# A two-layer image network on one core: layer 1's experts and final pass of three images placed within the last image's sampling

## The chip, the core and the metric

The kernel is one program on one core of a Trainium2 chip. The core has TensorE (PE, matrix products and transposes; its loads of the stationary operand are listed as PEld), VectorE (DVE), ScalarE (ACT), GpSimd (POOL) and SyncE (SP). Each has its own queue of instructions and runs it strictly in order. Memory transfers are issued from queues of SP, ACT and POOL and carried out by 16 DMA engines. The metric is the device time of one execution in microseconds (us), median over runs; lower is better. The profile is of one execution.

## The reference

The input is four images x of 128 channels by 128 x 128 pixels, all float32. There are two layers, each a convolution step and a mixture-of-experts step, both with residuals.

```
# layer 0
x = x + deform_conv(norm_over_channels(x))       # 9 taps, each at a learned offset, bilinear: 4 corners per tap
t = tokens(x)                                    # 16384 tokens of 128 per image
t = t + moe2(layernorm(t))                       # 8 experts, softmax router, the best 2 of each token
# layer 1
x = x + fourier_conv(norm_over_channels(x))      # real part of ifft2 of a channel mix of fft2
t = tokens(x)
z = layernorm(t)
probs = softmax(z @ gate_w.T + gate_b, over the 16384 tokens)      # 64 experts
topv, topi = the 8 tokens of largest probs, for each expert
pooled[e] = sum_k topv[k,e] * z[topi[k,e]]
out[e] = gelu([pooled[e],1] @ weight1[e]) ; out[e] = [out[e],1] @ weight2[e]   # 129x512 and 513x128 per expert
t[topi[k,e]] += topv[k,e] * out[e]               # scatter-add of 512 rows per image
x = image(t)                                     # back to channel-major
```

In layer 1 experts choose tokens, so no expert of an image can be run before all 16384 tokens of the image have been through the layers ahead of it. weight1 and weight2 are 16.8 MB each. The Fourier convolution reduces to x + A * (x flipped in both axes), and the kernel computes it so: `flip` and `aT_sb`.

## The kernel before, in words

**Sampling.** For each image a table in DRAM is built (`Image`, `block`, `positions`), whose row for a pixel holds the normalised pixel and its lower neighbour. One row read at a position, together with the next row, then gives all four corners of a bilinear sample. `Chunk.gather` issues three indirect DMAs on POOL for one image row and three taps; `weighted` multiplies the samples by the bilinear weights on DVE (`weighted_too` does the third tap of some chunks on ACT); `summed` adds the corners while transposing on PE (`trg`); `convolved` multiplies by the convolution weights (`sums`). A group is four image rows: two near the top and the two that mirror them, as the flip needs. It has 12 chunks. An image has 32 groups, thus 384 chunks, and the four images have 1536.

**Mixing.** `mixed` carries a group through layer 0's router and experts, the Fourier convolution, layer 1's layernorm and gate, and writes the tokens x2 to DRAM (`x2_d`). Of each run of tokens it keeps the best eight logits of each expert with their places (`best`, `best_at`). Experts of an even image lie in partitions 0 to 63, of an odd one in 64 to 127 (`gwT_sb[:, h]`), and `chosen(p)` picks the eight tokens of each expert for a pair of images, once the pair's second image is done.

**The order of work.** It is written out by hand. `InOrder` (its line, L83, is the line of every instruction that goes through it) keeps each engine's instructions in program order. `Turns` is a small cooperative scheduler that runs while the program is written: one slot per chunk, and jobs (generators) which say after how many slots they go on (`yield 1`, `yield turns.hop`), or wait for a free PSUM bank (`yield FILL`, at most `BANKS` = 6 over two adjacent slots). A chunk takes a bank itself. `turns.hop` is 2 while chunks run and 1 at the end: the slots between a matmul and the use of its result. Chunks are gathered `AHEAD` = 7 slots before they are summed, and there are as many gather buffers. While an image is sampled, the table of the next one is built (jobs `table_of`). In the last image's slots there is no table to build. SP carries the loads of x (`xc`, `xg`), the table writes (`table<-ent`) and the writes of x2.

**Behind the sampling.** When all slots are done, and the mixing of the last group too, comes straight-line code with pools of its own. `Pair` gathers the chosen tokens of two images (16 indirect DMAs, L1064), normalises and sums them weighted by their probabilities (L239, L1077, L1081), and puts them into `poolT`. The experts run once for all four images: 16 chunks of four experts. `first_layer` loads 1 MB of weight1 and four blocks of weight2 and multiplies (`ph`, L1165); `transposed` turns the hidden units and applies bias and gelu (`trh`, L1179); `second_layer` multiplies by weight2 (`po`, L1199); `turned` turns the outputs back (`pt`, L1211). Between them `Pair.equal` computes `share`, which for each chosen row adds up the weights of all experts that chose the same token (L1094 to L1105), so that rows chosen twice are written with the same sum. `Pair.give` adds the outputs to the gathered tokens and scatters them into `x2_d` (L1128). The final pass reads x2 in 64 tiles of 512 KB, transposes them (`pf`, L1248), copies them from PSUM on DVE and ACT and writes out (`ob`), the reads issued from SP, the writes from ACT.

Of the kernel before, what the change touches and what calls it, by code (L numbers as in the profile page):

```python
# [48 lines left out]
P = 128  # L50
NB = 4
# [6 lines left out]
TOPK = 8  # L58
TAPS = 9
# [5 lines left out]
TC = P + 2  # L65
AHEAD = 7
# [29 lines left out]
class Turns:  # L96
# [10 lines left out]
    def start(self, job, wait=0):  # L107
        self.jobs.append([job, self.slot + wait, False])
# [20 lines left out]
    def fills(self, spare):  # L129

        for one in self.jobs[:]:
            while one[2]:
                taken = sum(self.filled.get(self.slot - i, 0) for i in range(self.hop))
                if taken + spare >= BANKS or self.filled.get(self.slot, 0) + 2 >= BANKS:
                    return
                self.fill()
                if not self.resume(one):
                    break
# [30 lines left out]
def metaformer_kernel(  # L169
# [31 lines left out]
    x2_d = [dram.tile([2 * NTOK, P], F32, name=f"x2_d{p}") for p in range(NB // 2)]  # L201

    def x2_cols(b):

        half = x2_d[b // 2][b % 2 * NTOK : (b % 2 + 1) * NTOK, :]
        return half.rearrange("(x y) c -> x (y c)", y=P)
# [4 lines left out]
    best = [const.tile([P, RUNS, TOPK], F32, name=f"best{p}") for p in range(NB // 2)]  # L211
    best_at = [const.tile([P, RUNS, TOPK], U32, name=f"best_at{p}") for p in range(NB // 2)]

    token = [const.tile([P, TOPK], F32, name=f"token{p}") for p in range(NB // 2)]
    index = [const.tile([P, TOPK], I32, name=f"index{p}") for p in range(NB // 2)]
    val = [const.tile([P, TOPK], F32, name=f"val{p}") for p in range(NB // 2)]
    iota = const.tile([P, RUNS * TOPK], F32, name="iota")
    nmax = [const.tile([P, P // 4], F32, name=f"nmax{p}") for p in range(NB // 2)]
    esum = [const.tile([P, P // 4], F32, name=f"esum{p}") for p in range(NB // 2)]

    def rstd_of(pool, mv, n, eps, tag):

        r = pool.tile([P, n], F32, name=f"{tag}_rs", tag=f"{tag}_rs")
        nc.scalar.activation(r, mv[:, :, 1], AF.Sqrt, bias=eps)
        nc.vector.reciprocal(r, r)
        return r

    def layernorm(pool, src, dst, n, eps, tag):

        st = pool.tile([P, n, 6], F32, name=f"{tag}_st", tag=f"{tag}_st")  # L230
        mv = pool.tile([P, n, 2], F32, name=f"{tag}_mv", tag=f"{tag}_mv")
        for i in range(n):
            nc.vector.bn_stats(st[:, i, :], src(i))
            nc.vector.bn_aggr(mv[:, i, :], st[:, i, :])
        r = rstd_of(pool, mv, n, eps, tag)
        nb = pool.tile([P, n], F32, name=f"{tag}_nb", tag=f"{tag}_nb")
        nc.vector.scalar_tensor_tensor(nb, mv[:, :, 0], -1.0, r, ALU.mult, ALU.mult)
        for i in range(n):
            nc.scalar.activation(  # L239
                dst(i), src(i), AF.Identity, bias=nb[:, i : i + 1], scale=r[:, i : i + 1]  # L240
            )

    with ExitStack() as main:
        wts = main.enter_context(tc.tile_pool(name="wts", bufs=1))
        pa = main.enter_context(tc.tile_pool(name="pa", bufs=2))
        pt = main.enter_context(tc.tile_pool(name="pt", bufs=1))
        pw = main.enter_context(tc.tile_pool(name="pw", bufs=2))
        pg = main.enter_context(tc.tile_pool(name="pg", bufs=AHEAD))
        pb = main.enter_context(tc.tile_pool(name="pb", bufs=2))
        p_x = main.enter_context(tc.tile_pool(name="p_x", bufs=BANKS, space=PSUM))  # L250
# [13 lines left out]
        class Image:  # L264
# [23 lines left out]
            def border(self):  # L288
# [3 lines left out]
                    in_=zeros.rearrange("p (j e) -> p j e", j=2),  # L292
# [3 lines left out]
                    in_=zeros[0:1].rearrange("p (j e) -> p j e", j=2),  # L296
# [23 lines left out]
        zeros = wts.tile([P, 4 * P], F32, name="zeros")  # L320
# [8 lines left out]
        gwT_sb = wts.tile([P, 2, 2 * E1], F32, name="gwT_sb")  # L329
        nc.vector.memset(gwT_sb, 0.0)  # L330
        gb_sb = wts.tile([P, 1], F32, name="gb_sb")
        for h in range(2):
            nc.sync.dma_start(out=gwT_sb[:, h, h * E1 : (h + 1) * E1], in_=gate_w)
# [377 lines left out]
        def mixed(group):  # L711
# [7 lines left out]
            x1 = pb.tile([P, 4, P], F32, name="x1", tag="x1", bufs=5)  # L719
# [151 lines left out]
            p, h = divmod(b, 2)  # L871
            half = slice(h * E1, (h + 1) * E1)
            pq = bank([P, 4, P], "pq")
            eng.tensor.matmul(pq, lhsT=gwT_sb[:, h, :], rhs=tn2T, start=True, stop=True)
# [4 lines left out]
            eng.scalar.activation(lq[half], pq[half], AF.Identity, bias=gb_sb[half])  # L879
            yield 1  # L880
            tops = [best[p][half, (y + 1) // 2, :] for _, y, _ in runs]
            for i, (s, y, n) in enumerate(runs):
                run = lq[half, s : s + n, :].rearrange("p s c -> p (s c)")
                eng.vector.max(out=tops[i], in_=run)
                eng.vector.max_index(
                    out=best_at[p][half, (y + 1) // 2, :], in_max=tops[i], in_values=run
                )
            g = slice(group.number, group.number + 1)
            low = nmax[p][half, g]
            eng.vector.tensor_tensor(low, tops[0][:, 0:1], tops[1][:, 0:1], ALU.max)  # L890
            eng.vector.tensor_scalar(low, low, -1.0, None, ALU.mult)
            last = h == 1 and group.number + 1 == len(groups)
            exps.append((lq[half], low, esum[p][half, g], p if last else None))
# [4 lines left out]
        def exponentials():  # L898

            while exps:  # L900
                logits, low, total, pair = exps.pop(0)
                eng.scalar.activation(logits, logits, AF.Exp, bias=low, accum_out=total)
                if pair is not None:
                    turns.start(chosen(pair), 1)
# [391 lines left out]
```

## Time and profile before

| | us |
|---|---|
| median of 3 runs (6427.51 to 6435.13) | 6430.69 |
| the profiled execution's own time | 6432.53 |
| its span, first to last instruction | 6430.5 |
| busy PE / DVE / ACT / POOL over the span | 5722.3 / 5408.9 / 3801.4 / 4398.7 |
| mean granted TensorE clock | 0.957 of full |
| moved by DMA | 1488.42 MB, mean 231 GB/s |

How to read it: "busy" is the time in which an engine has an instruction in execution; issuing a DMA isn't counted, save for the indirect ones on POOL (`DMA_INDIRECT`), which show with their time of issue. In a row by stretch of time each engine has its busy time with the number of its instructions. In a row of waits come the instruction that waited, what released it, the total time, the number and the longest. "issue" as the releaser means that the profile shows nothing that the engine waited for. In a timeline row come the start, the duration, the engine, the line, the instruction, its count, and in brackets the idle time before it with its releaser. In a row of DMA issues come the destination and source, the queue, the number, the size and the median time from issue to landing.

The stages: the first image's table until about 150, the sampling of four images with the table of the next one beside it until about 6036, the last groups' mixing until about 6131, then choice, experts, scatter and final pass to 6430.5.

### The profile page before, as it was taken

The page shows a single profiled execution, that of the slowest core. Times are in us where ns is not written, and L with a number is a line of the kernel's source. Part 1 is how long each engine was busy: PE and PEld are TensorE (multiplying, and loading weights), DVE is VectorE, ACT ScalarE, POOL GpSimd, SP SyncE. Part 2 cuts the span into 40 slices and gives each one's busy share as a digit, 9 for nine tenths or more (in the row PEclk, how much of TensorE's full clock was granted, in tenths as well). Part 3 has the DMA queues.
Part 4 walks back from the last instruction along what each step waited for, and adds up shares of the span by engine and source line. Part 5 has one row for each costly group of instructions (what it writes and reads, how often), then busy time and mean ns, then how long its engine had stood idle before and what let it go on. Part 6 is the DMA issues. An engine that isn't in the chain of part 4 may idle for free.

```text
span 6430.5 us, 101708 instructions
## 1 busy us (share of the span) xinstructions
PE 5722.3 (89%) x30863; PEld 3750.9 (58%) x30863; DVE 5408.9 (84%) x16007; ACT 3801.4 (59%) x10144; POOL 4398.7 (68%) x4653
## 2 busy tenths in 40 slices
PE   8789999999899999999899999999888888888746
PEld 3456666666566666666565656666555555555425
DVE  5579988899899999899889998999888888888862
ACT  5456666665566666666566666666555555555522
POOL 0577777777777777777777777777777777777410
PEclk8899999999999999999999999999999999999976
DMA  4677877777777778777777777777777777777649
GB/s 138 198 238 242 249 236 237 234 226 224 237 243 243 240 242 249 225 227 226 238 244 237 243 239 237 239 236 226 220 224 220 224 223 221 224 221 224 201 160 405
DMA packets 580527, 1488.42 MB, mean 231 GB/s; under 512 B 84840, under 2 KB 251600, under 8 KB 579984
## 3 DMA queue, kind: packets, MB, share of 16 engines
q0 software_dynamic: 369664, 1210.35, 63.1%
q1 hardware_dynamic: 200944, 237.85, 10.8%
q10 hardware_dynamic: 9376, 33.72, 1.3%
q8 instruction: 250, 4.10, 0.3%
q14 instruction: 293, 2.40, 0.1%
HBM read 1344.74 MB, written 136.85 MB: 230 GB/s over the span
## 4 chain that ended last, share of the span: by engine, by line
PE 33%; DVE 33%; DMA 19%; issue 6%; ACT 4%; POOL 4%; POOLq 0%; SPq 0%; DVEq 0%; ACTq 0%
DMA g<-table,index 16%; PE trg L83 12%; DVE g L83 11%; DVE x L83 10%; PE sums L83 7%; PE pe L83 5%; PE po L83 5%; POOL g L83 4%; PE tr L83 2%; DMA out<-ob 2%; ACT ent L83 1%; DVE c_st L83 1%; DVE best_at L83 1%; ACT g L83 1%; PE ps L83 1%
## 5 line engine op out<-in xcount | busy, mean ns | idle before, releaser
L83 POOL DMA_INDIRECT g<-table,index x4608 | 4364.2, 947 | 1665.7 <-issue 836.0
L83 PEld LDWEIGHTS trg<-ident,g 128*128 128x128 f32 x18432 | 2132.4, 143 | 1157.4 <-issue 676.2
L83 PE MATMUL trg<-ident,g 128*128 128x128 f32 x18432 | 2359.5, 278 | 290.0 <-issue 117.2
L83 DVE TENSOR_TENSOR g<-g,spread 128x1024 f32<-128x1024 f32 (+1 forms) x1536 | 2136.2, 1392 | 346.7 <-DMA g<-table,index 312.6
L83 DVE SCALAR_TENSOR_TENSOR x<-pe,scaled,x 128x128 f32<-128x128 f32 x4096 | 1424.8, 348 | 196.7 <-PE pe L83 85.8
L83 ACT ACTIVATE g<-g,weight 128x128 f32<-128x128 f32 x4096 | 1306.9, 392 | 457.8 <-DMA g<-table,index 260.6
L83 PE MATMUL sums<-sT,wconv_sb 128*128 128x512 f32 x2304 | 1216.9, 610 | 0.2
L83 PE MATMUL pe<-ew_sb,x1T 128*128 128x512 f32 x2048 | 1087.9, 614 | 111.7 <-ACT sT L83 64.5
L83 ACT COPY sT<-trg 128x384 f32<-128x384 f32 x1536 | 713.0, 467 | 612.0 <-PE trg L83 608.9
L83 PEld LDWEIGHTS sums<-sT,wconv_sb 128*128 128x128 f32 x2304 | 406.7, 194 | 427.1 <-issue 424.4
L83 PEld LDWEIGHTS pe<-ew_sb,x1T 128*128 128x128 f32 x2048 | 318.8, 193 | 213.6 <-ACT sT L83 84.2
L83 PE MATMUL po<-pad,woff_sb 128*54 128x512 f32 x768 | 373.0, 627 | 7.4 <-ACT pad L83 5.0
L83 ACT ACT_TABLE_LOAD x264 | 338.7, 1283 | 22.0 <-DMA rw_sb<-in_router_w 8.4
L83 ACT ACTIVATE xn<-x,c_nb,c_rs 128x128 f32<-128x128 f32 x512 | 210.6, 483 | 111.2 <-DVE c_nb L83 111.0
L83 ACT ACTIVATE ent<-raw,a_nb,a_rs 128x128 f32<-128x128 f32 x512 | 210.6, 484 | 70.7 <-DVE a_nb L83 69.4
L83 ACT ACTIVATE tn<-x,d_nb,d_rs 128x128 f32<-128x128 f32 x512 | 211.0, 485 | 55.1 <-DVE d_nb L83 55.1
L83 PE MATMUL sums<-xg,ident 128*128 128x512 f32 x256 | 151.3, 675 | 97.5 <-ACT x1T L83 97.2
L83 PEld LDWEIGHTS po<-pad,woff_sb 128*54 128x54 f32 x768 | 93.8, 134 | 208.2 <-issue 189.8
L83 DVE BATCH_NORM_STATS2 a_st<-raw 128x6 f32<-128x128 f32 x512 | 137.5, 268 | 51.9 <-ACT raw L83 51.9
L83 ACT ACTIVATE e<-e 128x4 f32<-128x4 f32 x128 | 26.3, 206 | 259.8 <-DVE e L83 259.2
L1248 PE MATMUL pf<-ident,xt 128*128 128x128 f32 x512 | 114.2, 389 | 67.2 <-DVE ob L1250 33.6
L83 ACT COPY os<-po 54x512 f32<-54x512 f32 x128 | 74.1, 579 | 159.4 <-PE po L83 159.1
(208 smaller groups left out, 5310.0 us busy)
## 6 DMA issues: line engine op xcount, KB each, us to landing
g<-table,index POOLq DMA_INDIRECT x4608, 3.7
table<-ent SPq DMA_DIRECT2D x64, 1024.0 KB, 6.2
xc<-in_x SPq DMA_DIRECT2D x64, 512.0 KB, 6.7
xt<-x_d SPq DMA_DIRECT2D x64, 512.0 KB, 7.2
out<-ob ACTq DMA_DIRECT2D x64, 512.0 KB, 7.8
xg<-in_x SPq DMA_DIRECT2D x124, 256.0 KB, 5.4
x_d<-x SPq DMA_DIRECT2D x124, 256.0 KB, 4.0
w<-in_weight SPq DMA_DIRECT2D x16, 1024.0 KB, 8.8
```

The costliest lines, as they stand in the source:

```text
L83: return self.tc.keep_in_program_order(issue(*args, **kwargs))
L1248: nc.tensor.transpose(pf[:, i, :], xt[:, 4 * g + i, :], ident)
```

## The change

The token choice is made per image. The gate's weights stand in both halves of the stationary operand, so that both halves of the partitions hold the 64 experts' logits of the same image. Of an expert's best eight tokens the lower half keeps the first four and the upper half the last four (`KEPT`), so one indirect DMA still moves 128 rows, and an image needs four of them.

The code behind the sampling becomes jobs of the same scheduler, marked `later`: they get a free PSUM bank only after the others. `Experts` holds a set of images: `taken` gathers and pools, `network` runs both layers with one gelu between them, `give` scatters, `sent` is the final pass. One `Experts` for images 0 to 2 starts with the last image's first slot, in the space of the closed pools of the table building, with two buffers of 1 MB for weights and then for the final pass's tiles (`depth` 2, a first layer every two slots, `pace`). A second one, for image 3, starts when the last chunk is done, with nine such buffers in the space of the sampling's pools, and reads the weights again. `lead` spaces POOL's and the tiles' instructions by slots as long as chunks run, and sends the outputs by SP instead of ACT. weight2 is read in rows of 2 KB instead of 512 bytes: hidden unit number 4p + j is now in place (p, j). The buffers of x1 go from five to four, and the table's borders are zeroed from a source that is read twice.

```diff
+KEPT = TOPK // 2
+EC = 4
+NC = E1 // EC
+LATE = NB - 1
...
+    def start(self, job, wait=0, later=False):
+        self.jobs.append([job, self.slot + wait, False, later])
...
-        for one in self.jobs[:]:
+        for one in sorted(self.jobs, key=lambda one: one[3]):
...
+    x2_d = [dram.tile([NTOK, P], F32, name=f"x2_d{b}") for b in range(NB)]
...
+        phase_a, sampling = (main.enter_context(ExitStack()) for _ in range(2))
+        pa = phase_a.enter_context(tc.tile_pool(name="pa", bufs=2, side="right"))
+        pt = phase_a.enter_context(tc.tile_pool(name="pt", bufs=1, side="right"))
         pb = main.enter_context(tc.tile_pool(name="pb", bufs=2))
+        pw = sampling.enter_context(tc.tile_pool(name="pw", bufs=2))
+        pg = sampling.enter_context(tc.tile_pool(name="pg", bufs=AHEAD))
...
+        gwT_sb = wts.tile([P, 2 * E1], F32, name="gwT_sb")
...
-            x1 = pb.tile([P, 4, P], F32, name="x1", tag="x1", bufs=5)
+            x1 = pb.tile([P, 4, P], F32, name="x1", tag="x1", bufs=4)
...
+            eng.scalar.activation(lq, pq, AF.Identity, bias=gb_sb)
...
+            for h in range(2):
+                half, mine = slice(h * E1, (h + 1) * E1), slice(h * KEPT, (h + 1) * KEPT)
+                eng.vector.tensor_copy(place[half], i8[half, mine])
+                eng.vector.tensor_copy(top[half], m8[half, mine])
...
+        class Weights:
+            def __init__(self, room):
+                self.room, self.tiles, self.loaded = room, {}, 0
+            def load(self, upto):
+                while self.loaded < min(upto, 2 * NC):
+                    i = self.loaded
+                    layer, c = divmod(i, NC)
+                    some = slice(c * EC, (c + 1) * EC)
+                    self.tiles[i] = self.room(i)
+                    eng.sync.dma_start(
+                        out=self.tiles[i],
+                        in_=weight2[some, 0:HID, :].rearrange("e (p j) o -> p e (j o)", j=NJ)
+                        if layer
+                        else weight1[some, 0:P, :].rearrange("e d h -> d e h"),
+                    )
+                    self.loaded += 1
...
+            def lead(self):
+                return AHEAD + 2 if turns.hop > 1 else 0
+            def start(self):
+                turns.start(self.inputs(), later=True)
+                turns.start(self.network(), later=True)
...
+            def taken(self, b):
+                while b not in known:
+                    yield 1
+                yield self.lead()
+                tok = self.tok[b] = late.tile([P, KEPT, P], F32, name=f"tok{b}", tag=f"tok{b % LATE}", bufs=1)
+                for k in range(KEPT):
+                    eng.gpsimd.indirect_dma_start(
+                        out=tok[:, k, :],
+                        out_offset=None,
+                        in_=x2_d[b],
+                        in_offset=bass.IndirectOffsetOnAxis(ap=index[b][:, k : k + 1], axis=0),
+                    )
+                if self.lead():
+                    yield 4
...
+                eng.vector.tensor_tensor(
+                    tn, tn, val[b].unsqueeze(2).to_broadcast([P, KEPT, P]), ALU.mult
+                )
+                sum4 = late.tile([P, P], F32, name="sum4", tag="one")
+                eng.vector.tensor_reduce(sum4, tn.rearrange("p k c -> p c k"), AX.X, ALU.add)
+                yield 1
...
+                for k in range(KEPT):
+                    wide = late.tile([P, P], F32, name="wide", tag="one")
+                    eng.vector.tensor_copy(wide, token[b][:, k : k + 1].to_broadcast([P, P]))
+                    yield 1
+                    yield FILL
+                    along = bank([P, P], "along")
+                    eng.tensor.transpose(along, wide, ident)
+                    yield turns.hop
+                    same = late.tile([P, P, KEPT], F32, name="same", tag="two")
+                    eng.vector.tensor_tensor(
+                        same,
+                        along.unsqueeze(2).to_broadcast([P, P, KEPT]),
+                        token[b].unsqueeze(1).to_broadcast([P, P, KEPT]),
+                        ALU.is_equal,
+                    )
+                    eng.vector.tensor_tensor(
+                        same, same, val[b].unsqueeze(1).to_broadcast([P, P, KEPT]), ALU.mult
+                    )
+                    eng.vector.tensor_reduce(share[:, k, :], same, AX.X, ALU.add)
...
+                def first_layer(c):
+                    while c not in weights.tiles:
+                        yield 1
+                    yield FILL
+                    ph = bank([P, HID], "ph")
+                    w1 = weights.tiles.pop(c)
+                    for e in range(EC):
+                        at = m * (c * EC + e)
+                        eng.tensor.matmul(
+                            ph[32 * e : 32 * e + 32, :],
+                            lhsT=self.given[:, at : at + 32],
+                            rhs=w1[:, e, :],
+                            start=True,
+                            stop=True,
+                        )
+                    yield turns.hop
+                    weights.load(c + 1 + self.depth)
+                    hidden = late.tile([P, HID], F32, name="hidden", tag="hidden")
+                    eng.scalar.copy(hidden, ph)
...
+                def second_layer(c):
+                    while NC + c + 1 not in weights.tiles:
+                        yield 1
+                    yield FILL
+                    po = bank([P, 2, P], "po2")
+                    for i in range(2):
+                        w2 = weights.tiles.pop(NC + c + i)
+                        for j in range(NJ):
+                            for e in range(EC):
+                                at = m * ((c + i) * EC + e)
+                                eng.tensor.matmul(
+                                    po[32 * e : 32 * e + 32, i, :],
+                                    lhsT=self.units[:, j, at : at + 32],
+                                    rhs=w2[:, e, j * P : (j + 1) * P],
+                                    start=(j == 0),
+                                    stop=(j == NJ - 1),
+                                )
+                    yield turns.hop
+                    weights.load(NC + c + 2 + self.depth)
...
+                for c in range(NC):
+                    turns.start(first_layer(c), later=True)
+                    yield self.pace
+                while len(done) < NC:
+                    yield 1
+                some = self.units[:, :, 0 : E1 * m]
+                eng.scalar.activation(some, some, AF.Gelu)
+                yield 1
+                for c in range(0, NC, 2):
+                    turns.start(second_layer(c), later=True)
+                    yield 2 * self.pace
+                while len(done) < NC + NC // 2:
+                    yield 1
+                for b in self.bs:
+                    turns.start(self.give(b), later=True)
+                    yield self.pace
+                while len(done) < NC + NC // 2 + m:
+                    yield 1
+                tiles = [(b, t) for b in self.bs for t in range(P // RB)]
+                for i in range(self.depth):
+                    turns.start(self.sent(tiles[i :: self.depth]), later=True)
...
+            def sent(self, tiles):
+                for b, t in tiles:
+                    io = self.weights.room(t)
+                    xt, ob = io[:, 0:2, :], io[:, 2:4, :]
+                    some = slice(t * RB * P, (t + 1) * RB * P)
+                    eng.sync.dma_start(
+                        out=xt.rearrange("p i c -> p (i c)"), in_=x2_cols(b)[:, some]
+                    )
+                    done = []
+                    def part(g):
+                        yield FILL
+                        pf = bank([P, HID], "pf")
+                        for i in range(4):
+                            some = slice(i * P, (i + 1) * P)
+                            eng.tensor.transpose(pf[:, some], xt[:, g, some], ident)
+                        yield turns.hop
+                        if g == 0:
+                            eng.scalar.copy(ob[:, g, :], pf)
+                        else:
+                            eng.vector.tensor_copy(ob[:, g, :], pf)
+                        done.append(g)
+                    if self.lead():
+                        yield 2
+                    for g in range(2):
+                        turns.start(part(g), later=True)
+                    while len(done) < 2:
+                        yield 1
+                    if self.lead():
+                        yield 1
+                    (eng.sync if self.lead() else eng.scalar).dma_start(
+                        out=out_cm[b, :, some], in_=ob.rearrange("p i x -> p (i x)")
+                    )
...
+            if n == LATE * slots:
+                phase_a.close()
+                late = main.enter_context(tc.tile_pool(name="late", bufs=2, side="right"))
+                b1T = late.tile([P, NJ, E1], F32, name="b1T", tag="b1T", bufs=1)
+                b2T = late.tile([P, E1], F32, name="b2T", tag="b2T", bufs=1)
+                turns.start(biases(), later=True)
+                room = lambda i: late.tile([P, EC, HID], F32, name="w", tag="w")
+                weights = Weights(room)
+                weights.load(2)
+                Experts(range(LATE), weights, 2, 2).start()
...
+                sampling.close()
+                own = main.enter_context(tc.tile_pool(name="own", bufs=OWN))
+                room = lambda i: own.tile([P, EC, HID], F32, name="w", tag="w")
+                weights = Weights(room)
+                weights.load(OWN)
+                Experts(range(LATE, NB), weights, OWN, 1).start()
...
```

## The prediction

> **What bounds it now.** I read the page's table of busy tenths first, then busy times by stage, then the waits inside the last image's stage, then the timeline behind it. Busy times by stage (microseconds, busy PE, PEld, DVE, ACT, POOL, then granted clock, DMA share, GB/s):
>
> ```profile
> 3060.00:4520.00 1460.00, 1356.76 (x7409) 901.56 (x7408) 1322.92 (x3975) 930.27 (x2501) 1094.31 (x1155) 0.98 0.78 237
> 4520.00:5970.00 1450.00, 1261.54 (x6857) 834.79 (x6855) 1221.55 (x3421) 816.02 (x2194) 1096.83 (x1160) 0.99 0.75 222
> ...
> 6040.00:6127.00 87.00, 56.50 (x151) 27.26 (x150) 64.06 (x261) 38.82 (x77) 0.00 (x0) 0.77 0.48 157
> 6127.00:6166.00 39.00, 3.31 (x13) 1.64 (x17) 28.00 (x102) 13.96 (x28) 16.35 (x16) 0.50 0.11 31
> 6166.00:6242.00 76.00, 60.03 (x760) 33.67 (x752) 61.69 (x96) 19.02 (x51) 1.00 (x1) 0.90 0.86 277
> 6242.00:6263.00 21.00, 1.17 (x11) 0.97 (x9) 1.38 (x2) 0.00 (x0) 14.54 (x15) 0.61 0.14 47
> 6263.00:6431.00 168.00, 114.20 (x512) 86.24 (x512) 44.28 (x64) 37.52 (x64) 0.00 (x0) 0.63 1.00 401
> ```
>
> The second row is the last image's sampling, where no further table is built. It issues 1160 gathers in 1450 us: 1.25 us each, although POOL reads as only 76% busy. The waits of that stage (total us, times, longest) say why:
>
> ```profile
> POOL g L83 <- issue: 163.9, 538, 0.3
> ...
> DVE g L83 <- DMA g<-table,index: 126.1, 96, 4.0
> ```
>
> POOL's idle times are never longer than 0.3 us: a gather is 0.95 us plus 0.3 us to the next, so **POOL's issue rate is the bound** there, and DVE waits for gathers. PE is 87% busy, DVE 84%, ACT 56%. The first row (image 2 sampled, image 3's table built) has PE at 93%, DVE at 91%, and still 1.264 us per gather. Behind the sampling lie a drain (6036 to 6131, DVE's chain), choice and pooling, the experts, the scatter, and a final pass at DMA share 1.00: about 394 us with POOL idle.
>
> **Removed behind the sampling.** Only image 3 is left there.
> (a) Last logits maximum (6131.6) to first expert matmul (6165.3): 33.7 us for 16 token gathers and two pools. Then: 2 us of maxima, 4 rows of 0.82 us, 17 small DVE operations of 0.2 us, 4 gathers at 1.25 us and 2.5 us to land, statistics, 4 normalisations of 0.4 us, multiply, reduce, transpose: 23.5. **-10.**
> (b) Experts, 6165.3 to 6237.6: 72 us, DMA-bound. Then: nine of 32 loads (1 MB each) run in the drain; the other 24.1 MB at an estimated 380 GB/s (between this stage's best slices, 360 to 398, and the final pass's 415) take 63, with 4 for the last matmuls: 67. **-5.**
> (c) 6237.6 to 6262.6: 16 scatters, 25 us. Then: 3 us to the first, 4 x 1.27, 2.2 to land: 10.3. **-15.**
> (d) Final pass, 168 us for 67.3 MB. A quarter, 16.8 MB at 415 GB/s, is 40.4, plus the same 7 of fill and end: 47. **-121.**
> (e) The 1.8 us clearing of poolT, which sat in DVE's last chain: **-2.** Sum **-153**.
>
> **Added to the last image's sampling.**
> (f) POOL: 12 token gathers and 12 scatters at 1.25 us stand in the queue that is the bound: **+30**, which nothing hides.
> (g) A two-input multiply on DVE can hold POOL up. The row, in the timeline behind the sampling:
>
> ```profile
> 6149.76 0.94 POOL L1064 DMA_INDIRECT tok<-x_d,index  x1 [0.30 <-issue]
> 6151.01 1.56 POOL L1064 DMA_INDIRECT tok<-x_d,index  x1 [0.30 <-issue]
> ```
>
> The second ran beside the multiply of tn by val and took 0.62 us longer. The Trainium skill (SBUF — State Buffer, Who interferes with whom) says that a VectorE instruction with two SBUF inputs contends with a GpSimd instruction that reads SBUF, and the second to issue blocks. 15 such multiplies move in (3 tn, 12 same); the sampling's own multiply takes its weights from PSUM. Half as long as that row's, each can block some 0.6 us: 0 to 9, by row and rule together **+6**; if the rule didn't hold here, 0.
> (h) Engine work, from the timeline's rows at full clock (8 records of ph in 1.04 us, 8 of pf in 1.07). PE: ph 16 x 1.04, trh 16 x 0.66, po 16 x 1.08, pt 16 x 0.33, pf 384 x 0.134 at full clock, 12 along, 12 four and the rest some 11: 112 us. DVE: same 12 x 1.8, copies of pf 48 x 0.69, one more choice 10, tokens 14, units, outT and the rest: 87. ACT: 49 (hidden 9, copies of pf 28, the rest 12). Over 1476 us (1440 + f + g) PE comes to (1252 + 112)/1476 = 92%, DVE 88%: an image with a table, near enough, and that costs 0.014 us per gather, 16 us. I take **+12** (0 to 20). The cover is POOL's 0.25 us per gather in which PE has nothing to do; without it PE's 112 would show whole.
> (i) Weights: 33.6 MB through two buffers. A first layer needs two PSUM banks; sampling (12) and a group's mixing (16) take 28 of 36 in twelve slots, so first layers get about one per three slots (11 us), second layers a pair in four (15 us), for 2 MB. The nearest rows, from the DMA view of image 2's sampling:
>
> ```profile
> g<-table,index POOLq DMA_INDIRECT x947, 3.7
> table<-ent SPq DMA_DIRECT2D x14, 1024.0 KB, 5.6
> ...
> xc<-in_x SPq DMA_DIRECT2D x12, 512.0 KB, 8.1
> ```
>
> A 512 KB read beside the gathers needs 8.1 us, so 1 MB some 14, two abreast 10 each, about what the free 25% of DMA gives. By the row, second layers starve: 16 x 10 = 161 us against 120, +41, and first layers some +10. The rule (DMA: Bandwidth & Descriptors, Queues, rings and completion order) has each DMA engine alternate between queues packet by packet, so the load would get up to half: about 5 us per MB; no starving, but gathers then pay: demand 0.75 + 0.34 = 1.09 over 120 us, +11. Three to four spare gather buffers (some 13 us) absorb one such backlog. A ph that waits for its weights holds up the next chunk's trg on PE, then its buffer, then POOL's next gather. I take **+20**, nearer the rule because the gathers' landing was the same 3.7 us beside table writes and without (0 to 52).
> (j) Slots (one per chunk, 3.75 us; counted from the program's yields). Image 2's last group needs about 54 slots for its mixing, its exponential comes with a later group's, and the choice takes 10: ready about slot 78 of 384. Its tokens are pooled 21 later, at 99; first layers to 154, second to 188, scatters at 213. Two chains of 24 tiles then take some 7.5 slots per tile (load, 2, start, fill, 2 to the copy, 2 to the output): to slot 394, while the sampling's turn ends at 386. So about four tiles run in the drain, where transposes no longer lag their loads and PE waits for each: **+8** (0 to 30). Further back, token gathers and scatters are consumed 4 slots on while POOL is some 5 chunks behind: DVE waits about 8 us three times, within the spare buffers: 0.
> (k) SP gets 130 issues more (32 weights, 48 tiles in, 48 out, 2 biases), near 1 us each by its rows, in 1470 us. An output that waits for its copy, or a load for its buffer, holds up what is queued behind it: xg loads, which are issued some 10 slots ahead of PE's use, and x2 writes. Hidden by that lead; if a wait exceeded 35 us, the sampling would stop for the excess. The wider gate matmul and logits use all 128 partitions in the same time: 0. Image 1 gets a choice of its own, 10 us of DVE in a stage with table: **+4** (0 to 10). x1 with four buffers (held some 36 of 48 slots), borders from a broadcast, right-hand pools: 0.
> Sum **+80**.
>
> Net -73. The profiled execution took 6432.5 (span 6430.5 and 2.0 around it): 6360; the median of the runs, 6430.7, is 1.8 lower: **6358 us**.
>
> **Rivals.** *All hidden but POOL.* For: image 2's stage carries as much PE and DVE work at 1.264. Only f, g, k: 6430.7 - 153 + 40 = 6318. Against: the expert stage is bursty, the table isn't.
> *Network and drain congested.* Weights by the row (+52), h at 20, overrun 30 because first layers come late: +142, 6420. For: xc's 8.1 us. Against: the 25% of DMA that is free would just carry it.
> *Slower: the final pass's round trip through SP.* Both chains share two buffers; SP, in order, waits for A's output before A's next load, then for B's output before B's load. From the first output: two outputs, one load, two slots to the copies: 2 x 5.6 + 8.1 + 7.5 = 27 us against a round of 7.5 slots, 28.5; hidden. With outputs at the 9.2 us that the chain of waits shows for `out<-ob` in the final pass, 34: 24 x 5.5 = 132 more, which with the 80 makes 6490. It decides from about 31.5 us per round (24 x 3 = 73), outputs at 8 us. For: in-order SP with a wait on a write. Against: those 9.2 us were at DMA share 1.00; here it comes to some 0.93, and table writes of 1 MB landed in 5.6.
> *The change doesn't do what it says:* experts so late that most final tiles fall behind the sampling. 30 tiles x 2.6 us of DMA, half of it in the drain's idle DMA: about 6390; it lies inside the range.
>
> **Chances.** Forecast 0.52 (6335 to 6390), all hidden 0.18, congested (late experts too) 0.19, slower 0.11. A measurement can tell 0.2% (13 us) from no change. Faster: all but the slower case and a few hundredths of the congested one: 0.87; within 0.2%: 0.03; slower 0.10. Range: with only f of the added costs the time would be 6308, so it begins at 6305; it ends at 6432, past the congested case's 6420 and the slower case's point of decision, which leaves out some 0.03 below and 0.12 above.
>
> **What will show it.** f: 1176 POOL indirect DMAs from about 4594, still 0.3 us apart, the last near 6100. g: those beside `same` near 1.5 us. i: PE ph and po waiting for DMA w. j: pf of image 2 behind the last gather. a to e: last gather to end about 250 us. Wrong if POOL's waits for PE trg exceed some 60 us, or if SP's waits for out set the rounds.

## The result, and the profile after

| | us |
|---|---|
| before, median of 5 runs | 6428.59 (6427.07 to 6435.13) |
| after, median of 5 runs | 6395.08 (6389.48 to 6400.41) |
| ratio | 0.9946 [0.9931, 0.9960] |
| forecast | 6358 (6305 to 6432) |

The change gains 34 us where 73 were forecast: the direction holds, the gain is less than half of the forecast, and the time lies inside the range. The profiled execution after has a span of 6393.2 us against 6430.5, so these two executions differ by 37 us where the medians differ by 34. The same stages as in the views of before follow for the kernel after: image 3's sampling, the drain behind it in three pieces, the choice, the experts, the scatter and the final pass (busy PE, PEld, DVE, ACT, POOL, granted clock, DMA share, GB/s):

```profile
4593.00:6098.00 1505.00, 1310.60 (x7819) 903.63 (x7819) 1272.31 (x3571) 839.19 (x2253) 1113.86 (x1176) 0.96 0.80 259
...
6098.00:6150.00 52.00, 29.06 (x142) 18.84 (x141) 21.74 (x85) 17.66 (x43) 0.62 (x1) 0.77 0.70 260
6150.00:6200.00 50.00, 34.06 (x136) 20.39 (x134) 37.23 (x139) 17.77 (x35) 0.00 (x0) 0.80 0.54 183
6200.00:6250.00 50.00, 22.17 (x64) 11.44 (x64) 30.63 (x111) 25.04 (x47) 0.00 (x0) 0.70 0.11 37
6250.00:6270.00 20.00, 3.81 (x18) 0.96 (x18) 10.88 (x43) 2.53 (x6) 3.76 (x4) 0.50 0.05 13
6270.00:6337.00 67.00, 52.59 (x720) 30.72 (x716) 11.14 (x44) 13.73 (x26) 0.00 (x0) 0.89 0.95 362
6337.00:6350.00 13.00, 0.00 (x0) 0.00 (x0) 0.30 (x1) 0.00 (x0) 3.91 (x4) 0.61 0.17 44
6350.00:6393.00 43.00, 24.47 (x128) 21.33 (x128) 11.07 (x16) 9.18 (x16) 0.00 (x0) 0.66 0.96 383
```

The experts (67 us), the scatter (13) and the final pass (43, with 128 transposes in place of 512) look as the sum had them. The drain (from the last gather of the sampling to the last maximum of the logits) doesn't: it reaches to 6246, and its first 100 us move 260 and 183 GB/s. Cut exactly at the last gather's end and at the last maximum of the logits, the drains of before and after, in that order:

```profile
6033.10:6131.60 98.50, 64.26 (x196) 32.42 (x194) 74.41 (x292) 46.16 (x95) 3.15 (x4) 0.77 0.45 147
```

```profile
6098.60:6245.80 147.20, 84.69 (x336) 50.36 (x334) 85.03 (x321) 56.06 (x116) 0.02 (x1) 0.76 0.47 166
```

It is 48.6 us longer and has 140 PE records more. 100 of these are `pf`, the transposes of final tiles of images 0 to 2, at eight a tile: 12.5 tiles, where four were forecast. They are called late tiles below. Laid out by the steps of the prediction (profiled executions; the end of one row is the start of the next):

| stage | before | after | difference | forecast |
|---|---|---|---|---|
| to image 3's first gather (k) | 4592.6 | 4593.2 | +0.6 | +4 |
| image 3's gathers (f, g, h, i) | 1440.5 | 1505.5 | +65.0 | +68 |
| drain (j, e) | 98.5 | 147.1 | **+48.6** | +6 |
| last maximum to first `ph` (a) | 33.7 | 21.3 | -12.4 | -10 |
| experts (b) | 72.3 | 67.8 | -4.5 | -5 |
| scatter (c) | 25.0 | 12.7 | -12.3 | -15 |
| final pass (d) | 168 | 45.8 | -122.2 | -121 |
| sum | | | -37 | -73 |

**The drain alone is the miss:** 42.6 us over its forecast; all the other rows together are 7 under theirs. Two views of the kernel after say how it loses time. First PE's waits in the drain (total us, times, longest), then PE's timeline there (start, length; in brackets the wait and what ended it):

```profile
PE pf L90 <- DMA w<-x_d: 34.1, 6, 22.9
```

```profile
6143.11 1.94 PE L90 MATMUL pf<-ident,w 128*128 128x128 f32 x8 [22.94 <-DMA w<-x_d]
...
6182.43 1.62 PE L90 MATMUL pf<-ident,w 128*128 128x128 f32 x8 [2.65 <-DMA w<-x_d]
...
6203.17 1.87 PE L90 MATMUL pf<-ident,w 128*128 128x128 f32 x8 [4.00 <-DMA w<-x_d]
```

PE stands before the transposes of a tile that isn't there yet, once for 23 us. What was queued ahead of that tile is in SP's timeline of the same kernel:

```profile
6110.35 0.38 SPq L90 DMA_DIRECT2D w<-in_weight  x1
6110.83 0.45 SPq L90 DMA_DIRECT2D w<-x_d  x1
6111.33 0.43 SPq L90 DMA_DIRECT2D x_d<-x  x1
6111.81 19.16 SPq L90 DMA_DIRECT2D w<-in_weight  x8
6131.07 36.35 SPq L90 DMA_DIRECT2D w<-x_d  x5
```

A row of SP runs from its first issue to the end of its last. At the end of the sampling's turn (the slots in which the scheduler still places chunks) the kernel issues the last image's nine weight loads (`weights.load(OWN)`) on the queue from which the tiles come. SP is busy for 19.16 us with eight of them, which follow each other without a gap, and only then gets to the next tile, whose load takes another 12 us to land, to 6143. No one needs these weights before 6267. (The five tile loads of the last row are short; in its 36.35 us SP mostly waits for outputs to land and free a buffer, 61.3 us in all from 6131 to 6250.) PE carries out its instructions in order, as the 22.94 us show, so image 3's own tail of transposes stands behind the tile that PE waits for. And since `turns.hop` is 1 by then, `lead()` gives 0 and `sent` leaves out two waits, one of two slots between load and transposes and one ahead of the output: a further tile's transposes are put into PE's queue as soon as its load is issued.

The gathers came out near the forecast, but of other parts. POOL's waits from 4700 to 5900 of the kernel after:

```profile
POOL g L90 <- ACT sT L90: 15.4, 17, 9.9
POOL g L90 <- PE trg L90: 14.3, 24, 7.1
POOL x_d L90 <- DMA x_d<-tok,index: 14.1, 7, 2.6
```

Taken one by one, the +65.0 are 30 for the 24 further issues, 15.9 of gaps between scatters, 17.2 of waits for a free gather buffer (first two lines, less the usual 0.3 each; they lie between 5266 and 5352, in the second layers), and 1.9 for five gathers that took 1.2 to 1.43 us in place of 0.95. The 15.9 had not been thought of: before, scatters into two tensors, each of a pair of images, alternated and followed each other 0.30 us apart; after, four scatters into one image's tensor stand in a row, and each waits for the landing of the one ahead (POOL's timeline, before and then after):

```profile
6245.84 0.97 POOL L1128 DMA_INDIRECT x_d<-tok,index  x1 [0.30 <-DMA x_d<-tok,index]
6247.11 0.97 POOL L1128 DMA_INDIRECT x_d<-tok,index  x1 [0.30 <-DMA x_d<-tok,index]
```

```profile
5430.04 1.00 POOL L90 DMA_INDIRECT x_d<-tok,index  x1 [0.30 <-issue]
5433.40 0.98 POOL L90 DMA_INDIRECT x_d<-tok,index  x1 [2.36 <-DMA x_d<-tok,index]
5436.99 0.97 POOL L90 DMA_INDIRECT x_d<-tok,index  x1 [2.62 <-DMA x_d<-tok,index]
5439.49 0.96 POOL L90 DMA_INDIRECT x_d<-tok,index  x1 [1.54 <-DMA x_d<-tok,index]
```

### The profile page after: what moved, and what is told of

The parts are those of the page before. It is cut to its first block, busy times and chain, and to the rows that moved or that the text cites. A ratio compares the mean times of both kernels' runs of the same rounds, so it can differ in the third digit from the quotient of the medians.

```text
span 6393.2 us, 103261 instructions
## 1 busy us (share of the span) xinstructions
PE 5703.2 (89%) x31587; PEld 3771.2 (59%) x31587; DVE 5390.7 (84%) x16110; ACT 3789.7 (59%) x10155; POOL 4399.3 (69%) x4653
## 4 chain that ended last, share of the span: by engine, by line
PE 42%; DVE 29%; DMA 15%; issue 7%; ACT 4%; POOL 3%; SPq 0%; POOLq 0%; DVEq 0%; ACTq 0%
PE trg L90 15%; DMA g<-table,index 13%; DVE g L90 10%; DVE x L90 9%; PE sums L90 9%; PE pe L90 7%; PE po L90 6%; POOL g L90 3%; PE tr L90 3%; ACT ent L90 1%; PE ps L90 1%; ACT g L90 1%; DVE c_st L90 1%; DMA w<-in_weight 1%; DVE best_at L90 1%
## 5 line engine op out<-in xcount | busy, mean ns | idle before, releaser
L90 ACT COPY spread<-weight 128x72 f32<-128x72 f32 (+1 forms) x272 | 59.5, 219 | 186.2 <-DVE g L90 170.1
L90 DVE BATCH_NORM_STATS2 c_st<-x 128x6 f32<-128x128 f32 x512 | 151.0, 295 | 17.6
```

The costliest lines, as they stand in the source:

```text
L90: return self.tc.keep_in_program_order(issue(*args, **kwargs))
```

## The experiments

The theory to start with: the late tiles cost the drain some 40 us, by SP's order (the weights ahead of them) and the lost lag (the waits left out in `sent`); the rival: the drain is long for another reason (the last image's own chain, the weights' traffic), and the tiles only fill its gaps. All edits are to the kernel after.

**Four single edits.**

*No late tiles* (`sent` stops where the sampling's turn has ended):

```
                 for b, t in tiles:
+                    if self.depth == 2 and turns.hop == 1:
+                        return
```

> Leaves out the tiles of images 0 to 2 that would start their load after the last chunk (some 11 of 48, whose output is not written); all else stays. Theory (the tiles that spill into the drain stretch it, by PE waiting in order for their loads): the time from the last gather's issue to the last nmax falls from 147 us to about 100, the total by 40 to 47, to about 6350. Rival (the drain is long because nine weight loads stand on SP ahead of the x2 writes, or because its own chain grew): the drain stays above 130, the total falls by less than 15.

*The weights behind the drain's loads:*

```
-                weights.load(OWN)
+                turns.start(fetch(weights), 44)
...
+        def fetch(weights):
+            weights.load(OWN)
+            yield 1
```

> Only the nine weight loads of the second set are issued 44 slots later, behind the spilled tiles. If the 23 us wait of PE for a tile is due to SP's issuing of those loads (19 us for eight) ahead of the tile's load: the drain falls by 15 to 23 us, the total to about 6375. If the spilled tiles cost by their own round trip (load, transposes, output) whatever stands ahead: less than 6 us.

*The lag kept* (the same at both waits in `sent`):

```
-                    if self.lead():
+                    if self.depth == 2 or self.lead():
```

> The spilled tiles keep their two slots between load and transposes, and the one before the output, in the drain too. If PE's in-order wait on tiles without a lag is the cost: the drain falls by 10 to 25 us, the total to about 6375. If SP's queue of weight loads is: less than 6 us, the first wait of 23 us stays.

*Scatters spread* (in `give`, behind each scatter of the loop):

```
+                    if self.lead():
+                        yield 1
```

> One slot between the four scatters of an image while chunks run, so that three gathers stand between two scatters. Theory (each scatter waits for the landing of the one before it, 1.5 to 2.6 us, in the queue that is the bound): POOL's waits for x_d fall from 14 us to 0, the last gather comes 16 us earlier; the final pass starts 3 slots later, which spills about one tile more, +4; the total falls by 12, to about 6383. Rival (POOL would have waited there anyway for buffers): no change.

These four ran on a chip where the kernel before took 7490.89 us, 17% more than on the others, and where POOL's issue was not the bound of the sampling (see the last section); the kernel after was not run there, so I read the drains alone, and not against 147.1 but among themselves.

| | time | ratio to before, there | drain |
|---|---|---|---|
| no late tiles | 7421.09 | 0.9909 [0.9893, 0.9926] | 108.9 |
| weights later | 7437.80 | 0.9934 [0.9918, 0.9951] | 125.2 |
| lag kept | 7441.45 | 0.9937 [0.9920, 0.9953] | 128.3 |
| scatters spread | 7441.71 | 0.9937 [0.9920, 0.9953] | 141.2 |

The order is the theory's: the shortest drain without late tiles, 16 to 19 us more with one of the two causes removed, 32 more with neither. In the fourth run the gaps between scatters went from the 14.8 us of the three others to 0. What that is worth couldn't be read here: its gathers took 1780 us and those of the others 1790 to 1798, but POOL waits for buffers for over 300 us on this chip in any case. So the set was repeated elsewhere, with a control.

**The control, and the late tiles again.**

> The changed kernel itself, as the row to which the other three of this set are compared on the same chip: 147 us from the last gather to the last nmax, 12 scatters of images 0 to 2 at 2.5 to 3.6 us each.

> The edit of e1_no_late_tiles again (it leaves out some 11 tiles of images 0 to 2), beside the changed kernel on the same chip. Theory: last gather to last nmax 100 to 108 us instead of 147, total 38 to 45 below the changed kernel. Rival (the drain grew by itself): under 15 below.

Before took 6426.66 us there, the control 6398.18 (0.9954 [0.9938, 0.9971]), without late tiles 6352.52 (0.9882 [0.9866, 0.9899]). The two drains, control first:

```profile
6100.80:6247.80 147.00, 86.64 (x344) 52.08 (x342) 86.55 (x325) 57.02 (x118) 0.00 (x0) 0.75 0.47 167
```

```profile
6101.70:6205.10 103.40, 70.30 (x258) 38.00 (x256) 78.24 (x312) 50.72 (x108) 0.04 (x1) 0.79 0.36 135
```

Without them the drain is 43.6 us shorter, the time 45.7, and the gathers as they were (1510.6 and 1511.6). PE's waits for tiles in the control's drain are gone here:

```profile
PE pf L90 <- DMA w<-x_d: 34.5, 7, 22.6
```

The rival falls: the late tiles were the loss. By the `pf` records the control has 13 tiles in its drain. Ten tiles are not sent at all here, so their own work is gone with their waits; the other 2.5 or so, whose loads were issued before the turn ended, still run there. About 5 us of drain over the 98.5 of before stay, which no run took apart.

**One cause at a time, on a third chip,** where before took 6424.89:

> The edit of e2_weights_later again: the nine weight loads alone, 44 slots later. The changed kernel had 147 us from the last gather to the last nmax, 103 without spilled tiles. If SP's queue of weight loads is half of the cost of spilling: about 125; if none: above 140.

> The edit of e3_lag_kept again: the lags of spilled tiles alone are kept in the drain. If PE's in-order wait without a lag is half of the cost of spilling: about 128; if none: above 140. With e7 this tells whether the two add up to the 44 us.

Weights later gave 6370.56 (0.9909 [0.9894, 0.9924]) with a drain of 119.7, the lag kept 6375.07 (0.9919 [0.9903, 0.9934]) with 122.1: 27 and 25 us less than the control's 147.0 on the second chip (by the ratios, 29 and 22 us faster than the control). PE's waits in the drain, weights later first:

```profile
PE pf L90 <- DMA w<-x_d: 16.4, 8, 3.5
```

```profile
PE pf L90 <- DMA w<-x_d: 25.6, 4, 17.5
```

With the weights out of the way the long wait is gone and eight short ones are left; with the lag kept the tiles wait in a row no more, but the one behind the weights still takes 17.5. Together the two would make 52, more than the whole loss of 43.6: they overlap, and the shares of each can't be added. Both at once come next.

**All three edits in one** (weights later, lag kept, scatters spread):

> One slot between scatters, lags kept in the drain, weight loads 44 slots later. Theory: the last gather 16 us earlier (scatters no longer wait), the drain 20 to 30 us shorter: total 35 to 45 below the changed kernel. If the three edits remove the same wait twice, or the scatters' wait was hidden: 15 to 25.

6346.53 (0.9875 [0.9859, 0.9892]), 51.7 below the control beside it, more than expected. The drain is 112.6, 34.4 less, with 13 tiles in it as in the control; PE's waits for tiles in it are down to 2.0 us. It is still 9 us longer than without late tiles. The gathers take 1495.7 in place of 1510.6, for the scatters now have a gather between them (POOL's timeline):

```profile
5431.95 1.00 POOL L90 DMA_INDIRECT x_d<-tok,index  x1 [0.31 <-issue]
5433.26 0.97 POOL L90 DMA_INDIRECT g<-table,index  x1 [0.30 <-issue]
...
5437.03 0.99 POOL L90 DMA_INDIRECT x_d<-tok,index  x1 [0.30 <-issue]
```

These 14.9 us answer to the 15.9 of gaps between the control's scatters, of which 1.7 are left (one scatter still waits for the one ahead): while POOL's issue is the bound, a wait for a landing on its queue costs its full length.

**Shorter tiles.** The three edits, and a tile's two halves as one job instead of two that are started one after the other (the old `part` goes too, and the wait ahead of the transposes is three slots in place of two; cut):

```
-                    for g in range(2):
-                        turns.start(part(g), later=True)
-                    while len(done) < 2:
-                        yield 1
+                    halves = []
+                    for g in range(2):
+                        yield FILL
+                        pf = bank([P, HID], "pf")
+                        for i in range(4):
+                            part = slice(i * P, (i + 1) * P)
+                            eng.tensor.transpose(pf[:, part], xt[:, g, part], ident)
+                        halves.append(pf)
+                    yield turns.hop
+                    eng.scalar.copy(ob[:, 0, :], halves[0])
+                    eng.vector.tensor_copy(ob[:, 1, :], halves[1])
```

> As v3, and a tile of images 0 to 2 takes six to seven slots instead of nine (transposes, copies and output in one job), so that 48 tiles fit before the last chunk. Theory: no tile spills, drain about 100 us, total 55 to 65 below the changed kernel, near 6335 on a chip like the first. Rival (the round through SP, two outputs and a load in order, now sets the pace and PE waits for tiles within the sampling): PE waits over 40 us for tile loads before the last gather, total no better than v3's.

6343.67 (0.9873 [0.9857, 0.9890]): no difference from the run ahead of it that could be told. That no tile would be left for the drain was wrong: 9.5 are. Nor did the rival's wait come: PE has no wait for a tile's load from 4700 to 5900. But this run shows what a round (one tile on each of the two chains) takes. The records of `pf` (PE, PEld, copies on DVE and ACT) in the same stretch, kernel after and then this one:

```profile
5700.00:6060.00 360.00, 23.39 (x164) 18.89 (x164) 13.73 (x20) 11.55 (x20) 0.96 0.86 281
```

```profile
5700.00:6060.00 360.00, 30.50 (x200) 23.62 (x200) 17.10 (x25) 14.65 (x25) 0.99 0.88 293
```

Eight records a tile on two chains: 20.5 tiles are 35.1 us a round, 9.0 slots of 3.9 us; 25 tiles are 28.8 us, 7.4 slots. The 7.5 slots of the prediction hold for one job per tile; two jobs cost a slot and a half more. And with 9.5 tiles in its drain this kernel takes 106.0 us for it, against 103.4 with 2.5: in one execution of each, seven tiles more cost 2.6 us.

**The weights through two buffers.** The last edit slows the second layers of the first pass, on top of the four:

```
-                    yield 2 * self.pace
+                    yield (3 if self.m > 1 else 2) * self.pace
```

> As v4_short_tiles, and the second layers start every six slots instead of four, for 2 MB of weights each. Theory (POOL's 17 us of waits in the second layers' stretch come from PE waiting in order for weights through two buffers at a share of DMA near 1, until the spare gather buffers are used up): POOL's waits above 0.35 us fall from 17 to under 5, the last gather comes 12 to 17 us earlier, about four tiles more spill, total 5 to 15 below v4. Rival (PE's own added work fills the stretch, not the weights): the waits stay above 12.

6327.74 (0.9844 [0.9829, 0.9859]). POOL's waits for a buffer from 4700 to 5900, without this edit and with it:

```profile
POOL g L90 <- PE trg L90: 18.7, 29, 9.0
POOL g L90 <- ACT sT L90: 13.8, 16, 8.8
```

```profile
POOL g L90 <- PE trg L90: 8.5, 28, 0.3
POOL g L90 <- ACT sT L90: 4.6, 15, 0.3
```

PE's wait for `po`'s weights (19.4 us in the kernel after, 18.4 without this edit) is gone from its list, and the gathers take 1475.0 in place of 1493.1. That is the chain that step i described: a late weight holds up PE, PE the buffers, the buffers POOL. The edit also spreads PE's own work on the second layers over more slots, and no run parted the two; but the wait for weights that went is as long as the time gained (18.4 and 18.1). The gathers are now 34.5 us over those of before. 30 are step f's issues, about 2 longer gathers, 1.8 a scatter that still had to wait for the one ahead, and 0.7 a wait of one gather: for further engine work (step h) nothing is left.

**The best version.** All of these, but the last image's own tiles, which have no sampling to share with, keep their two jobs:

> As e6_second_slower, and image 3's own tiles keep the two separate jobs of the changed kernel, since in v4 the time from the last scatter to the end was 55 us instead of 48. Theory: 6 to 8 us below e6; 65 to 75 below the changed kernel on the same kind of chip.

6318.10 us in five runs (6317.57 to 6326.96), ratio to before 0.9834 [0.9821, 0.9848]: it beats both kernels, by 107 and, by the ratios (0.0112 of 6425), by about 72 us. 12 tiles are in its drain, which takes 105.3 us all the same (at a granted clock of 0.89, against 0.79 in the run without late tiles). Image 3's sampling, its drain and the rest:

```profile
4587.00:6062.00 1475.00, 1313.40 (x7878) 900.67 (x7877) 1272.68 (x3578) 838.49 (x2260) 1115.08 (x1177) 0.98 0.82 265
6062.50:6167.80 105.30, 70.26 (x299) 39.38 (x297) 82.68 (x317) 53.07 (x110) 0.03 (x1) 0.89 0.50 171
6167.80:6315.80 148.00, 81.78 (x862) 53.07 (x862) 37.10 (x115) 29.27 (x54) 7.70 (x8) 0.71 0.82 316
```

## Why the prediction was right or wrong

**Steps a to e, the gain: right.** Forecast -151 without (e), measured -151.4. Only the scatter is 2.7 short: its four, too, wait for each other, 2.5 us each in place of the 1.27 of before, where two tensors alternated.

**Steps f, g, h, i, the gathers: right in the sum, by luck: its parts offset each other.** +65.0 against 68. (f) 30, as worked out. (g) 2 in place of 6: the blocking shows where a gather begins while such a multiply runs, at seven of the 15, and beside two similar instructions of the choice (`junk`). The gather at 4841.02 began under a multiply of `same` that ended at 4841.63, and took 1.43 us. These nine gathers all ended 0.82 us after the instruction that they began under, thus 0.03 to 0.48 us late; gathers that began ahead of the multiply kept their 0.95. (h) nothing in place of 12: PE at 87% of this stage (1310.6 of 1505) still kept ahead of POOL, and DVE at 85% too. (i) 17 in place of 20, by the mechanism named and in the stretch named, though at another rate: the 1 MB loads landed in a median 8.1 us, between the row's estimate of 10 to 14 and the rule's 5. A term put at nothing: 16 us of scatters that wait for each other. Step c's row showed scatters 0.30 us apart, and I carried it over without asking why they could be so close; that the order of the issues had changed was in the diff.

**Step j, the slots: the step that failed.** Its mechanism was right (tiles spill into the drain, where their transposes no longer lag the loads, and PE waits) and its size was not: +8 forecast, within 0 to 30, +43.6 measured. Three terms were off. The number: 7.5 slots for a tile were 9.0, because its two halves are started as separate jobs; with the first transposes at slot 223 (counted by the `trg` records behind them), and the gathers' end at 384, that leaves 12.5 tiles for the drain, not four. The price of one: 2 us were put, and the ten that the run without late tiles left out had cost 43.6, 4.4 each. And the reason for the price: SP was looked at in step k for its number of issues, not for what stands in its queue at the end of the turn. Nine weight loads there hold up the tiles behind them; taking them away gave 27 us, the lag 25, both at once 34. With both causes gone 13 tiles still cost some 9 us over the run without late tiles; with a tile as one job besides, 12 of them cost 2 us in the best version. So the number alone was not the trouble. It shows in the sign that was named for it: from the last gather to the end 294.6 us, not about 250.

**The rivals.** *All hidden but POOL* (6318) was wrong for this kernel: i and the scatters showed on POOL and j in the drain. *Congested* (6420) had the drain's part (+30 there, 44 measured) and not the network's (17, not 52). *The final pass's round trip through SP* didn't come within the sampling: outputs landed in a median 4.9 us and tiles in 6.2 (DMA view of the kernel after, 5600 to 6000), against the 8 and more for outputs that it needed:

```profile
out<-w SPq DMA_DIRECT2D x24, 512.0 KB, 4.9
w<-x_d SPq DMA_DIRECT2D x24, 512.0 KB, 6.2
```

And from the 673rd of image 3's gathers on, through the whole of the final pass, the gathers run at a constant 65.9 us behind those of before. *Doesn't do what it says* gave about 6390, near the measured time, but not for its reason: 35.5 of 48 tiles were sent within the sampling, and the rest cost waits, not DMA.

## What to carry to other kernels

Work that is moved into the shadow of a longer stage needs a second look at the seam where that stage ends: what is left over runs there without its spacing, and queues up behind whatever the next phase prefetches on the same in-order queue; a load that no one needs for 150 us belongs behind one that is needed now. Count a round of cooperative jobs by what starts what, not by its waits alone. And where a queue is the bound, don't put two writes to the same tensor next to each other on it: with three other issues between them the wait for the landing was hidden here in all but one place.

## What the hardware showed that wasn't expected

But for the 17 us of step i, the heavy stretch of weights passed without harm. The DMA view of the kernel after from 5000 to 5300, size and median time to landing:

```profile
w<-in_weight SPq DMA_DIRECT2D x24, 1024.0 KB, 8.1
g<-table,index POOLq DMA_INDIRECT x240, 5.3
```

The gathers landed in 5.3 us in place of 3.7, at a DMA share of 0.89, and no wait of POOL that a gather's landing ended was longer than the usual 0.3 us. I read this as the work of the spare gather buffers; no run changed their number.

One chip ran the kernel before in 7490.89 us where the two others of these sets gave 6426.66 and 6424.89. Traces from it are of the edited kernels alone. In that with the weights later, an image took some 1721 us instead of the 1462 of before, and in 1700 us of it PE stood idle ahead of `trg` for 104.6 us with no releaser in the trace, against 10.9 us of 1400 in the control. The granted clock of the kernel before was 0.889 to 0.896 over the span there, and 0.955 to 0.961 on the two others: were PE the limit throughout, that would make some 7% of the 17%. For the rest no cause was found, and none was tried. A change's worth can differ between such chips: in image 3's sampling POOL waited for buffers for some 300 us there and 17 us here, so that what is saved in POOL's issue counts on one and need not on the other.
